# A GRU with a residual on one core: biases spread by products with ones, and x turned by VectorE in 32 x 32 squares

## The chip, the core and the metric

The kernel runs on one core of a Trainium2 chip. The core has TensorE (matrix products, results in PSUM), VectorE, ScalarE and GpSimd (elementwise work; GpSimd does not touch PSUM here), and SyncE (SP), which issues most DMAs. Each engine works through its own list of instructions in order, and waits for others through semaphores. The metric is device microseconds for one execution: the median of three runs before the change is 1333.65 us (1333.27 to 1333.81).

## What is computed

x has 64 rows (batch), 128 steps and 512 features. A GRU runs over the steps; after every fourth step the state goes through one more layer; the states are added to x.

```python
def step(h, inp):
    x_t, prop = inp
    comb = jnp.concatenate([x_t, h], axis=-1)
    z = jax.nn.sigmoid(comb @ Wz + bz)
    r = jax.nn.sigmoid(comb @ Wr + br)
    comb2 = jnp.concatenate([x_t, r * h], axis=-1)
    h_cand = jnp.tanh(comb2 @ Wh + bh)
    h_new = (1.0 - z) * h + z * h_cand
    h_next = jnp.where(prop, jnp.tanh(h_new @ Wp + bp), h_new)
    return (h_next, h_new)
...
x = x + _L0_cond_ref(x, cond_1024, ...)
```

All numbers are float32. The weights are 1024 x 512 for each of r, z and h, and 512 x 512 for the layer after every fourth step.

## The kernel before

**Layout.** The 64 batch rows fill half of the 128 partitions; the 512 features are cut in two halves (S = 2), so a state is a tile of 128 x 256: partition s*64+b, 256 columns of half s. A product takes as stationary operand a 128 x 64 piece of a turned (feature-major) state or x, and streams 256 columns of weights; two such products, one for each half of the columns, run side by side (`products`, L194 in the profile).

**Work of a step.** The recurrent part of a step is a chain: product of h with Wr's lower half (`rc`), sigmoid on ScalarE, r*h on VectorE (`rh`, L742), turning rh on TensorE in 64 x 64 pieces (`turn`, L219) with a copy out of PSUM (`rhT`, L210), product with Wh (`rc` again), tanh (L802), two VectorE operations that make the new state (L803, L808), and turning that (`hT`). Products with Wz (`zp`), the `keep` product (L769) and seeds (`seed`, L411: ScalarE copies the x part of the next step into PSUM, on which the recurrent products accumulate) stand between.

**Work in the gaps.** The x part, x @ W[:512] + b for all three gates, doesn't depend on h. It stands in a `queue` of small units, and `fill(n)` puts n of them wherever the chain would leave TensorE without work. Steps 0 to 3 and the last four are plain products (`plain`, `plain_last`). The others are formed for groups of four steps by two nested levels of a seven-product scheme (`batch`): sums of turned x tiles (`four`, `sum_*`, on GpSimd) times sums of weights (`tw`, `tt`), collected from four PSUM banks (`scratch_q`, `_r`, `_a`, `_x`) by ScalarE and VectorE (`end_1`, `end_2`, L541 to L552), put together by GpSimd (L582, L586, with the biases). `read_out()` places these collecting operations. Which units go where is written out by hand (`PLACES`, `TAIL`).

**How x gets turned.** Steps 0 to 7 are turned on TensorE (`turn_x`) from `xr`, the tile of x to which the state is added later. Steps 8 to 127 take another way, a group of four steps at a time: a load of x with batch rows on partitions (`load_xs`, and `early` for groups 2 and 3), a copy that parts each float32 into its two 16-bit words (`words_x`: GpSimd, L210; ScalarE for groups 2 and 3), a DMA transpose of 16-bit words (`planes_x`, L273), and a ScalarE copy that joins the words again (`join_x`, L283). In a regular period of eight steps two groups pass: joins stand in the steps u = 1, 3, 5, 6, one behind the seeds that follow rh (`join(0)`), one behind `keep` (`join(1)`).

**Start.** SP's ring brings, in this order: half of x of steps 0 and 1, the upper weight halves (`wx`, one piece of Wr and the other half of x through ScalarE's queue), the lower halves (`wh`) of r, of z, x of steps 2 and 3, `wh` of h, x of steps 4 to 7, `early`, Wp. A DMA waits for the one eight places ahead of it to finish. GpSimd's queue brings the state h0 and the biases br, bz, bh, each as two DMAs that repeat one line of 256 numbers on 64 partitions (`load_bias`, L121), after `held`, a copy of one number that waits for x (L130). TensorE first does products of zeros (`idle`), turns steps 0 and 1, then does the x part of steps 0 and 1 gate by gate (R, Z, candidate), turns h0 ahead of the candidate, and enters the loop over steps.

Of the kernel before, what the change touches and what calls it, by code (L numbers as in the profile page):

```python
# [9 lines left out]
F32 = mybir.dt.float32  # L10
BF16 = mybir.dt.bfloat16
U16 = mybir.dt.uint16
# [5 lines left out]
def kernel(  # L18
# [29 lines left out]
    nc = tc.nc  # L48
    B, T, D = x.shape
    H = h0.shape[1]  # L50
    P = 128
    S = 2
    N = H // S
    C = N // P
    K = D // P
    Q4 = 4
# [3 lines left out]
    R, Z, H_ = range(3)  # L60
# [4 lines left out]
    one = ctx.enter_context(tc.tile_pool(name="one", bufs=1))  # L65
    xtp = ctx.enter_context(tc.tile_pool(name="xt", bufs=2))
    mbp = ctx.enter_context(tc.tile_pool(name="mb", bufs=3))
# [8 lines left out]
    ones = const.tile([1, B], F32, name="ones")  # L76
# [5 lines left out]
    wx = const.tile([P, K, 3, H], F32, name="wx")  # L82
# [3 lines left out]
    tw = {n: const.tile([P, S, S, 3, P], F32, name=f"tw_{n}") for n in (2, 3, 4)}  # L86
    tt = const.tile([P, 7, 3, S, 3, P // 2], F32, name="tt")
    gates_in = (Wr, Wz, Wh)
    def load_x(tile_, t0, n, j=0):
        for s in range(S):  # L90
            nc.sync.dma_start(
                out=tile_[s * B : (s + 1) * B, j : j + n, :], in_=x[:, t0 : t0 + n, ts(s, N)]
            )

    def load_w(wt, w, k0, k1, eng):
        eng.dma_start(  # L96
            out=wt[:, k0:k1, :],
            in_=w[k0 * P : k1 * P, :].rearrange("(k p) n -> p k n", p=P),
        )

    xr = {}
# [5 lines left out]
    bias_in = const.tile([P, 4, N], F32, name="bias")  # L107
    new_xr(0)
    for s in range(S):
        (nc.sync, nc.scalar)[s].dma_start(  # L110
            out=xr[0][s * B : (s + 1) * B, 0:2, :], in_=x[:, 0:2, ts(s, N)]
# [7 lines left out]
    def load_bias(i, eng):  # L119
        for s in range(S):  # L120
            eng.dma_start(  # L121
                out=bias_in[s * B : (s + 1) * B, i, :],
                in_=(br, bz, bh, bp)[i][ts(s, N)]
                .rearrange("(o n) -> o n", o=1)
                .broadcast_to([B, N]),
            )


    held = const.tile([1, 1], F32, name="held")
    nc.gpsimd.tensor_copy(held, xr[0][0:1, 0, 0:1])  # L130
    for s in range(S):
        nc.gpsimd.dma_start(out=h_init[s * B : (s + 1) * B, :], in_=h0[:, ts(s, N)])
    for i in (R, Z, H_):
        load_bias(i, nc.gpsimd)
    for i in range(3):
        for k in (0, 2):
            load_w(wh[i], gates_in[i][D:, :], k, k + 2, nc.sync)
        if i == Z:
            load_x(xr[0], 2, 2, 2)

    dummy = const.tile([1, 1], F32, name="dummy")
    nc.scalar.activation(dummy, ones[:, 0:1], AF.Sigmoid)
    new_xr(1)
    load_x(xr[1], 4, 4)
    early = {}
    for g in (2, 3):
        early[g] = mbp.tile([P, 2, 2, 3, P], F32, tag="mb", name=f"early_{g}").rearrange(
            "p a b c d -> p (a b c d)"
        )[:, : Q4 * N].rearrange("p (t n) -> p t n", t=Q4)
    load_x(early[2], 8, 4)  # L150
    load_w(wp, Wp, 0, 4, nc.sync)
    load_bias(3, nc.sync)
    load_x(early[3], 12, 4)


    rc = ps_c.tile([P, 2, N], F32, name="rc")
# [3 lines left out]
    scratch = [ps_c.tile([P, 2 * N], F32, name=f"scratch_{n}") for n in "qrax"]  # L160
# [9 lines left out]
    bias = bias_in.rearrange("p i (c n) -> p c i n", c=C)  # L170

    def cut(ps):
        return ps.rearrange("p (c n) -> p c n", c=C)

    bias0 = bias[:, 0, 0:3, :]
    bias_d = const.tile([P, 3, P], F32, name="bias_d")
# [32 lines left out]
    def copy(eng, dst, src):  # L209
        (eng.copy if eng is nc.scalar else eng.tensor_copy)(dst, src)  # L210

    def turn(src, dst, c, name, eng):


        pt = turn_ps[c][:, :P].bitcast(BF16).rearrange("p (w n) -> p w n", w=2)
        for s in range(S):
            words = src[:, c * P + s * B : c * P + (s + 1) * B].bitcast(BF16)
            for w in range(2):
                nc.tensor.transpose(  # L219
                    pt[s * B : (s + 1) * B, w, :],  # L220
                    words.rearrange("p (n w) -> p w n", w=2)[:, w, :],
                    ident16,
                )
        copy(
            eng,
            dst[:, c, :].bitcast(U16).rearrange("p (n w) -> p n w", w=2),
            pt.bitcast(U16).rearrange("p w n -> p n w"),
        )
# [3 lines left out]


    xT = {}
    xs = {}
    xw = {}
    xv = {}

    def new_xT(g):
        if g not in xT:  # L240
            xT[g] = xtp.tile([P, Q4, C, P], F32, tag="xT", name=f"xT_{g}")

    def turn_x(t, eng=nc.scalar):
        g, i = divmod(t, Q4)
        new_xT(g)
        src = xr[g] if g < 2 else early[g]
        for c in range(C):
            turn(src[:, i, :], xT[g][:, i], c, f"xT_{t}", eng)

    def load_xs(g):  # L250
        if g * Q4 < T:
            xs[g] = one.tile([P, Q4, N], F32, tag="xs", name=f"xs_{g}")
            load_x(xs[g], g * Q4, Q4)

    def words_x(g, i):

        if g * Q4 >= T:
            return
        if g not in xw:
            xw[g] = one.tile([P, Q4, 2, N], U16, tag="xw", name=f"xw_{g}")  # L260
        src = (early if g < 4 else xs)[g]
        copy(
            nc.scalar if g < 4 else nc.gpsimd,
            xw[g][:, i],
            src[:, i, :].bitcast(U16).rearrange("p (n w) -> p w n", w=2),
        )

    def planes_x(g):

        if g * Q4 >= T:  # L270
            return
        xv[g] = one.tile([P, Q4, 2, C, P], U16, tag="xv", name=f"xv_{g}")
        nc.sync.dma_start_transpose(  # L273
            out=xv[g].rearrange("p t w c n -> p (t w c) n"),
            in_=xw[g].rearrange("p t w n -> p (t w n)"),
        )

    def join_x(g, i):

        if g * Q4 >= T:  # L280
            return
        new_xT(g)
        nc.scalar.copy(  # L283
            xT[g][:, i].bitcast(U16).rearrange("p c (n w) -> p w c n", w=2), xv[g][:, i]
        )


# [129 lines left out]
    def fill(n):  # L417
        for _ in range(min(n, len(queue))):
            unit, end = queue.pop(0)
            unit()  # L420
            if end is not None:
                pending.append(end)

    def read_out():
        while pending:
            pending.pop(0)()
# [223 lines left out]
    idle(4)  # L650
    turn_x(1, nc.vector)
    idle(8)
    nc.gpsimd.tensor_sub(bias_d, bias[:, 1, 0:3, :], bias0)
    h = h_init
    hT = new_T("hT", "hT_init")
    both = [plain(0), plain(1)]
    for e in range(3):
        for us in both:
            queue.extend(us[4 * e : 4 * e + 4])
        fill(4)  # L660
        if e == H_:
            read_out()
            seed(R, 0)
            seed(Z, 0)
            seed(H_, 0)
        fill(4)
        if e == Z:
            for c in range(C):
                turn(h, hT, c, "hT_init", nc.vector)
# [4 lines left out]
    for t in range(T):  # L674
        g, j = divmod(t, Q4)
        prop = j == CHUNK - 1 and t < T - 1
        last = t == T - 1
        pair, u = divmod(t - 3, 8)
        even, odd = FIRST + 2 * pair, FIRST + 2 * pair + 1
# [43 lines left out]
        for k in ORDER:  # L723
            product(slots[R], hT, wh[R], k)
        if t < 2:
            if t:
                turn_x(6)
        if t == 1:
            for i in (5, 7):
                sum_inner(i, nc.gpsimd)  # L730
# [20 lines left out]

        for k in ORDER[: 2 if thin else 3]:
            product(slots[Z], hT, wh[Z], k)
        if t == 0:
            turn_x(2)
        rhT = new_T("rhT", f"rhT_{t}")
        for c in range(C):
            turn(rh, rhT, c, f"rhT_{t}", nc.vector)
# [17 lines left out]
        if t == 0:  # L776
            sum_outer()
            for i in (6,):
                sum_inner(i, nc.gpsimd)
                sum_inner_1(i, nc.gpsimd)  # L780
        if t == 1:
            for n in range(4):
                words_x(2, n)
            planes_x(2)
        elif t == 2:
            for n in range(1, 4):
                join_x(2, n)
            for n in range(2):
                words_x(3, n)
        if not thin:  # L790
            fill(places[0])
        if t == 0:
# [7 lines left out]
        for c in range(C):  # L800
# [3 lines left out]
            if last:  # L804
                o = xr[g][:, j, ts(c, P)]
# [2 lines left out]
            nc.vector.tensor_add(h_new[:, ts(c, P)], pc, keep[:, ts(c, P)])  # L808
        if t < T - 2:
            seed(H_, t + 1)  # L810
        if t == 2:
            for n in range(2, 4):
                words_x(3, n)
            planes_x(3)
        read_out()
        fill(places[0] if thin else 5 if places[1] > 6 else 4)
        if t == 1:
# [2 lines left out]
        h = h_new  # L820
# [15 lines left out]
        if prop:  # L836
# [3 lines left out]
            h = two.tile([P, N], F32, tag="hprop", name=f"hprop_{t}")  # L840
# [51 lines left out]
            sum_s12(even + 2)  # L892
        if t == 2:
            pair_right(0, 1, 10)
        if pair >= 0:
            if u in (1, 2):
                for n in range(2):
                    words_x(even + 2, 2 * (u - 1) + n)
            if u in (5, 6):
                for n in range(2):  # L900
                    words_x(odd + 2, 2 * (u - 5) + n)

        if not last:
            nc.gpsimd.tensor_add(xr[g][:, j, :], xr[g][:, j, :], h_new)  # L904
# [4 lines left out]
        n = 0  # L909
        if t >= T - CHUNK:  # L910
            n = {T - 2: 3, T - 1: 1}.get(t, 0)
        elif j == Q4 - 1:
            n = 4
        if n:
            for s in range(S):
                eng = nc.scalar if last and s else nc.sync
                eng.dma_start(
                    out=out[:, t - n + 1 : t + 1, ts(s, N)],
                    in_=xr[g][s * B : (s + 1) * B, j - n + 1 : j + 1, :],
                )  # L920
        if j == 1 and g >= 1 and (g + 1) * Q4 < T:
            new_xr(g + 1)
            load_x(xr[g + 1], (g + 1) * Q4, Q4)
        if t == 0:
            load_xs(4)
        if pair >= 0:
            if u == 3:
                planes_x(even + 2)
                load_xs(odd + 2)
            elif u == 6:  # L930
                planes_x(odd + 2)
                load_xs(even + 4)


# [37 lines left out]
```

## Time and profile before

| | us |
|---|---|
| median of three runs | 1333.65 |
| the profiled execution | 1334.15 |
| its span, first to last instruction | 1332.3 |

| group (line, engine) | count | mean ns | busy us |
|---|---|---|---|
| recurrent product with rhT, L194 TensorE | 2048 | 379 | 246.0 |
| copy of rhT out of PSUM, L210 VectorE | 256 | 420 | 97.6 |
| joining words, L283 ScalarE | 120 | 765 | 91.4 |
| parting words, L210 GpSimd | 112 | 613 | 65.3 |
| adding the state to x, L904 GpSimd | 127 | 728 | 92.5 |
| DMA transposes, issued by SP | 30 | 4.3 us to landing | |

TensorE rows are modelled durations of pipelined matmuls that overlap, so differences between starts are read, not sums of durations. The granted TensorE clock is 0.999 of full speed over the whole span. In the timeline a row has the start in us, the time from the start of the first to the end of the last of the merged instructions, engine, line, operation, output<-inputs, shapes, count, and in brackets the idle time before it and what ended it.

### The profile page before, as it was taken

Reading aid. Unit: us, or ns where it says so; the run is one execution under the profiler, and the core shown is the slowest. Engines: PE = TensorE matmul, PEld = TensorE weight load, DVE = VectorE, ACT = ScalarE, POOL = GpSimd, SP = SyncE. Lnnn points to the kernel's source line nnn. Section 1 sums busy time; section 2 is a strip of 40 time slices with the busy share of each in tenths; the row PEclk is TensorE's granted clock in tenths of the full one; section 3 lists DMA queues with packets and bytes.
Section 4 is the critical chain, followed back from the end, with each engine's and each line's share of the span. In section 5 each row is a group of like instructions: output and inputs, shape, how many; then the busy total and the mean of one; then the engine's idle time right before and its main releaser. Section 6 shows DMA issues by size and latency. Waiting matters only on the chain.

```text
span 1332.3 us, 37617 instructions
## 1 busy us (share of the span) xinstructions
PE 1321.7 (99%) x15320; PEld 1110.8 (83%) x15320; DVE 702.6 (53%) x1870; ACT 635.4 (48%) x1860; POOL 934.9 (70%) x1139
## 2 busy tenths in 40 slices
PE   8999999999999999999999999999999999999998
PEld 5788888888888888888788888888888888888765
DVE  3555555555555555555555555555555555555444
ACT  1554454454544544545444454545545444554433
POOL 4877876777777668776787767786777687767400
PEclk9999999999999999999999999999999999999999
DMA  9322232131221222213122221223212222131300
GB/s 283 55 49 49 49 65 64 33 65 41 57 65 33 66 52 46 65 44 82 37 43 55 64 65 33 59 40 65 65 33 65 49 50 65 33 76 37 98 23 17
DMA packets 119277, 77.79 MB, mean 58 GB/s; under 512 B 65984, under 2 KB 114240, under 8 KB 119104
## 3 DMA queue, kind: packets, MB, share of 16 engines
q1 hardware_dynamic: 118352, 74.14, 24.7%
q8 instruction: 121, 1.98, 0.6%
q10 hardware_dynamic: 496, 0.72, 0.2%
q0 software_dynamic: 256, 0.52, 0.1%
q14 instruction: 52, 0.43, 0.1%
HBM read 42.86 MB, written 16.78 MB: 45 GB/s over the span
## 4 chain that ended last, share of the span: by engine, by line
PE 96%; DMA 2%; DVE 1%; ACT 1%; issue 0%; SPq 0%; DVEq 0%; ACTq 0%
PE rc L194 33%; PE zp L194 20%; PE scratch_q L194 11%; PE scratch_r L194 10%; PE scratch_x L194 10%; PE scratch_a L194 6%; PE turn L219 5%; DMA xr<-in_x_dram 1%; DMA wx<-in_L_cond_Wz_dram 1%; ACT xw L210 0%; ACT xT L283 0%; DVE h L808 0%; DVE turn L803 0%; SPq L96 0%; DVE mb L550 0%
## 5 line engine op out<-in xcount | busy, mean ns | idle before, releaser
L194 PE MATMUL rc<-wh,rhT 128*64 128x256 f32 x2048 | 246.0, 379 | 0.0
L582 POOL TENSOR_TENSOR cp<-mb,mb 128x768 f32<-128x768 f32 x74 | 134.4, 1817 | 102.4 <-ACT rc L411 54.7
L194 PE MATMUL zp<-wh,hT 128*64 128x256 f32 x1536 | 204.3, 379 | 0.0
L194 PEld LDWEIGHTS rc<-wh,rhT 128*64 128x64 f32 x2048 | 168.3, 137 | 40.5
L194 PE MATMUL rc<-wh,hT 128*64 128x256 f32 x1536 | 186.3, 383 | 0.2
L904 POOL TENSOR_TENSOR xr<-xr,h 128x256 f32<-128x256 f32 x127 | 92.5, 728 | 105.3 <-DVE h L808 105.3
L194 PEld LDWEIGHTS rc<-wh,hT 128*64 128x64 f32 x1536 | 121.1, 137 | 36.5 <-issue 9.7
L582 POOL TENSOR_TENSOR cp<-mb 128x768 f32<-128x768 f32 x46 | 83.5, 1815 | 95.1 <-ACT rc L411 93.7
L210 DVE COPY rhT<-turn 128x256 uint16<-128x256 uint16 x256 | 97.6, 420 | 82.2 <-PE turn L219 81.1
L194 PEld LDWEIGHTS zp<-wh,hT 128*64 128x64 f32 x1536 | 118.8, 137 | 25.2
L803 DVE TENSOR_TENSOR turn<-turn,z 128x128 f32<-128x128 f32 x256 | 75.5, 295 | 120.7 <-ACT turn L802 119.0
L741 ACT ACTIVATE turn<-rc 128x128 f32<-128x128 f32 x256 | 55.2, 260 | 171.2 <-issue 111.5
L210 ACT COPY hT<-turn 128x256 uint16<-128x256 uint16 x127 | 47.3, 372 | 165.7 <-DVE hT L210 127.8
L582 POOL TENSOR_TENSOR mb<-mb,mb 128x768 f32<-128x768 f32 x58 | 105.3, 1816 | 9.6 <-DVE mb L552 9.6
L411 ACT COPY rc<-cp 128x256 f32<-128x256 f32 x256 | 96.4, 377 | 26.7 <-DVE cp L436 13.6
L550 DVE TENSOR_TENSOR mb<-scratch_r,cq 128x384 f32<-128x384 f32 (+1 forms) x105 | 58.3, 555 | 92.7 <-ACT cq L549 92.7
L802 ACT ACTIVATE turn<-rc 128x128 f32<-128x128 f32 x256 | 55.5, 260 | 105.3 <-PE rc L194 104.0
L543 DVE TENSOR_TENSOR cx<-scratch_r,cx 128x384 f32<-128x384 f32 (+1 forms) x105 | 58.3, 556 | 88.8 <-ACT cx L541 88.8
L767 ACT ACTIVATE z<-zp 128x256 f32<-128x256 f32 x128 | 49.1, 383 | 94.3 <-PE zp L194 94.2
L283 ACT COPY xT<-xv 128x512 uint16<-128x512 uint16 x120 | 91.4, 765 | 0.0
L808 DVE TENSOR_TENSOR h<-turn,keep 128x128 f32<-128x128 f32 x254 | 74.1, 292 | 15.6 <-DVE turn L803 0.5
L219 PEld LDWEIGHTS <-h 128*64 128x64 bf16 x1016 | 67.6, 110 | 14.0 <-DVE h L808 7.4
(161 smaller groups left out, 3018.0 us busy)
## 6 DMA issues: line engine op xcount, KB each, us to landing
xr<-in_x_dram SPq DMA_DIRECT2D x62, 256.0 KB, 4.1
out_dram<-xr SPq DMA_DIRECT2D x62, 256.0 KB, 3.4
xs<-in_x_dram SPq DMA_DIRECT2D x56, 256.0 KB, 4.2
wx<-in_L_cond_Wz_dram SPq DMA_DIRECT2D x2, 512.0 KB, 8.1
wx<-in_L_cond_Wh_dram SPq DMA_DIRECT2D x2, 512.0 KB, 11.4
wh<-in_L_cond_Wr_dram SPq DMA_DIRECT2D x2, 512.0 KB, 13.2
wh<-in_L_cond_Wz_dram SPq DMA_DIRECT2D x2, 512.0 KB, 15.2
wh<-in_L_cond_Wh_dram SPq DMA_DIRECT2D x2, 512.0 KB, 12.3
```

Of the source, the lines that this page charges most:

```text
L194: nc.tensor.matmul(ps[s * B : (s + 1) * B], lhsT=lhs, rhs=rhs(s), start=start, stop=True, skip_group_check=True,)
L210: (eng.copy if eng is nc.scalar else eng.tensor_copy)(dst, src)
L219: nc.tensor.transpose(pt[s * B : (s + 1) * B, w, :], words.rearrange("p (n w) -> p w n", w=2)[:, w, :], ident16,)
L283: nc.scalar.copy(xT[g][:, i].bitcast(U16).rearrange("p c (n w) -> p w c n", w=2), xv[g][:, i])
L411: nc.scalar.copy(cut(slots[i]), G[t][:, :, i, :])
L543: nc.vector.tensor_add(T2[n][:, :nm], r_ps[:, :nm], T2[n][:, :nm])
L550: nc.vector.tensor_add(blocks()[:, :nm, 0, 1], r_ps[:, :nm], q2[:, :nm])
L582: nc.gpsimd.tensor_add(dst, a, b)
L802: nc.scalar.activation(pc, slots[H_][:, ts(c, P)], AF.Tanh)
L803: nc.vector.tensor_mul(pc, pc, z[:, ts(c, P)])
L808: nc.vector.tensor_add(h_new[:, ts(c, P)], pc, keep[:, ts(c, P)])
L904: nc.gpsimd.tensor_add(xr[g][:, j, :], xr[g][:, j, :], h_new)
```

## The change

Three things change. The biases br, bh and bz come as single lines of 512 numbers (2 KB each) on GpSimd's queue into a corner of `tt` that isn't in use yet; behind the first eight units of the x part, `spread` makes four products of a column of ones with these lines, and ScalarE copies the results to `bias_in`. `held` now waits for a piece of Wr. x of steps 2 and 3 is loaded ahead of Wz's lower half, and step 2 is turned before the Z product instead of behind it. For x of steps 8 to 127, `load_xs` loads pieces of 32 numbers, so that each square of 32 batch rows by 32 features lies in the quarter of the partitions where its turned form belongs, and `join_x` is that one VectorE operation; `words_x`, `planes_x` and the `early` tiles go. There are two such load tiles instead of one, and the load of group 4 moves from step 0 to step 2.

```diff
+    bias_row = tt.rearrange("p a b c d e -> p (a b c d e)")[0:1, : 3 * H].rearrange(
+        "p (i n) -> p i n", i=3
+    )
...
+    for i, b in enumerate((br, bh, bz)):
+        nc.gpsimd.dma_start(out=bias_row[:, i, :], in_=b.rearrange("(o n) -> o n", o=1))
...
-    nc.gpsimd.tensor_copy(held, xr[0][0:1, 0, 0:1])
+    nc.gpsimd.tensor_copy(held, wx[0:1, 1, R, 0:1])
...
-    for i in (R, Z, H_):
-        load_bias(i, nc.gpsimd)
...
-        if i == Z:
+        if i == 0:
             load_x(xr[0], 2, 2, 2)
...
+    def load_xs(g):
+        if g * Q4 < T:
+            xs[g] = one.tile([P, Q4, S * C, 2, 32], F32, tag=f"xs{g % 2}", name=f"xs_{g}")
+            for r in range(4):
+                for bh in range(2):
+                    nc.sync.dma_start(
+                        out=xs[g][ts(r, 32), :, :, bh, :].rearrange("p t k e -> p (t k) e"),
+                        in_=x[ts(bh, 32), g * Q4 : (g + 1) * Q4, :].rearrange(
+                            "b t (k r e) -> r b (t k) e", k=S * C, r=4
+                        )[r],
+                    )
+    load_xs(2)
     load_w(wp, Wp, 0, 4, nc.sync)
     load_bias(3, nc.sync)
-    load_x(early[3], 12, 4)
+    load_xs(3)
...
+    def spread(bank, rows, which):
+        bank = bank.rearrange("p (i n) -> p i n", i=2)
+        n = len(which)
+        for s in range(S):
+            nc.tensor.matmul(
+                bank[s * B : (s + 1) * B, 0:n, :],
+                lhsT=ones,
+                rhs=bias_row[:, rows, ts(s, N)],
+                start=True,
+                stop=True,
+            )
+        for j, i in enumerate(which):
+            nc.scalar.copy(bias_in[:, i, :], bank[:, j, :])
...
     def join_x(g, i):
         if g * Q4 >= T:
             return
         new_xT(g)
-        nc.scalar.copy(
-            xT[g][:, i].bitcast(U16).rearrange("p c (n w) -> p w c n", w=2), xv[g][:, i]
+        nc.vector.transpose(
+            out=xT[g][:, i].rearrange("p c (s b) -> p s c b", s=S),
+            in_=xs[g][:, i].rearrange("p (s c) h e -> p s c (h e)", s=S),
         )
...
-    nc.gpsimd.tensor_sub(bias_d, bias[:, 1, 0:3, :], bias0)
...
         fill(4)
+        if e == R:
+            spread(scratch[3], slice(0, 2), (R, H_))
+            spread(scratch[1], slice(2, 3), (Z,))
+            nc.gpsimd.tensor_sub(bias_d, bias[:, 1, 0:3, :], bias0)
...
         if t < 2:
-            if t:
-                turn_x(6)
+            turn_x((2, 6)[t])
...
-        if t == 0:
-            turn_x(2)
...
-        if t == 1:
-            for n in range(4):
-                words_x(2, n)
-            planes_x(2)
-        elif t == 2:
+        if t == 2:
             for n in range(1, 4):
                 join_x(2, n)
-            for n in range(2):
-                words_x(3, n)
...
-        if t == 0:
+        if t == 2:
             load_xs(4)
         if pair >= 0:
             if u == 3:
-                planes_x(even + 2)
                 load_xs(odd + 2)
             elif u == 6:
-                planes_x(odd + 2)
                 load_xs(even + 4)
```

More of the change, by code (lines that the diff above doesn't have):

```diff
@@ L144 @@
     load_x(xr[1], 4, 4)
[L145 to L150, printed above, removed]
+    xs = {}
+    def load_xs(g):
[10 more added lines that the diff above has]
+    load_xs(2)
     load_w(wp, Wp, 0, 4, nc.sync)
     load_bias(3, nc.sync)
-    load_x(early[3], 12, 4)
+    load_xs(3)
     rc = ps_c.tile([P, 2, N], F32, name="rc")
@@ L234 @@
     xT = {}
-    xs = {}
-    xw = {}
-    xv = {}
     def new_xT(g):
@@ L245, in turn_x @@
         new_xT(g)
-        src = xr[g] if g < 2 else early[g]
+        src = xr[g]
         for c in range(C):
             turn(src[:, i, :], xT[g][:, i], c, f"xT_{t}", eng)
[L250 to L276, printed above, removed]
     def join_x(g, i):
@@ L810 @@
             seed(H_, t + 1)
[L811 to L814, printed above, removed]
         read_out()
@@ L894 @@
             pair_right(0, 1, 10)
[L895 to L901, printed above, removed]
         if not last:
```

## The prediction

> **What bounds the kernel now.** I read the engine row and the chain first, then the windows of the start, TensorE's timeline there, and last VectorE's timeline in a middle step.
>
> ```profile
> PE 1321.7 (99%) x15320; PEld 1110.8 (83%) x15320; DVE 702.6 (53%) x1870; ACT 635.4 (48%) x1860; POOL 934.9 (70%) x1139
> ...
> PE 96%; DMA 2%; DVE 1%; ACT 1%; issue 0%; SPq 0%; DVEq 0%; ACTq 0%
> ```
>
> The chain that ended last is TensorE, 96%. Sixteen matmuls of one 256-column product take 1.73 us, back to back, with no DMA, VectorE or ScalarE row ahead of them. So work removed from GpSimd, ScalarE or the DMA rings is worth nothing in itself; only holes in TensorE's row are. They lie at the start:
>
> ```profile
> 11.32 0.60 PE L194 MATMUL scratch_q<-wx,xT 128*64 128x256 f32 x4
> 12.44 1.52 PE L194 MATMUL scratch_q<-wx,xT 128*64 128x256 f32 x12 [0.52 <-DMA wx<-in_L_cond_Wz_dram]
> ...
> 20.16 1.51 PE L194 MATMUL rc<-wh,hT_init 128*64 128x256 f32 x12 [0.28 <-DMA wh<-in_L_cond_Wr_dram]
> 21.95 0.65 PE L194 MATMUL zp<-wh,hT_init 128*64 128x256 f32 x4 [0.28 <-DMA wh<-in_L_cond_Wz_dram]
> 23.73 1.08 PE L194 MATMUL zp<-wh,hT_init 128*64 128x256 f32 x8 [1.13 <-DMA wh<-in_L_cond_Wz_dram]
> 24.98 0.42 PE L219 MATMUL turn<-ident,xr 128*64 128x128 bf16 x8 [0.17 <-DMA xr<-in_x_dram]
> 25.75 0.58 PE L219 MATMUL turn<-ident,rh 128*64 128x128 bf16 x8 [0.35 <-ACT xT L210]
> ```
>
> Until 26.6 us TensorE waits for weights; the last one, the second half of Wz's recurrent rows, comes at 23.7. From there it is fed. How fast the weights come is in the windows (last two columns: share of the DMA engines, GB/s):
>
> ```profile
> 10.00:12.00 2.00, 1.93 (x18) 1.01 (x14) 0.00 (x0) 0.00 (x0) 0.00 (x0) 1.00 1.06 278
> 12.00:14.00 2.00, 1.56 (x14) 1.06 (x16) 0.00 (x0) 0.00 (x0) 0.00 (x0) 1.00 1.04 261
> 14.00:16.00 2.00, 2.00 (x28) 1.35 (x24) 0.15 (x1) 0.00 (x0) 0.99 (x1) 1.00 1.05 379
> ```
>
> The engines are full throughout, but carry 261 to 278 GB/s while GpSimd's queue (h0 and six bias pieces, issued from 4.3 us, bias_d waiting for them until 14.8) is at work, and 379 after it.
>
> **The biases.** Removed: six 64 KB pieces, 393 KB. At 379 GB/s their bytes alone are 1.0 us of the weights' way. From 8 to 14 us the three windows carried (327+278+261) x 2 = 1732 KB where 379 would have carried 2274: a further 1.4 us lost, three quarters of it the biases' share of that queue (384 of 512 KB), 1.1 us. Together 1.0 to 2.1; I take 1.9. Added ahead of the same transfer: x of steps 2 and 3 now goes before Wz's recurrent rows, 262 KB at the 287 GB/s of 20 to 22 us, 0.9 us. So the 23.7 us become 23.7 - 1.9 + 0.9 = 22.7; with nothing freed 24.6.
>
> The spreading costs TensorE two 512-column and two 256-column products on one row. No such row is in the trace. By columns, at 1.73 us for eight calls of 256, it is 6 x 0.216 = 1.30 us; if one row were cheaper, less, but matmul rows here follow their columns (379 ns at 256, 326 at 192), so 1.3. It stands where the wait at 12.44 is. TensorE's own schedule: 11.33 + 1.30 + 3.46 (Z) + 0.22 (h0 turned) + 3.46 (candidate) + 1.73 (R) + 0.22 (x of step 2, moved ahead) + 0.43 = 22.15 when it asks for the second half. That comes at 22.7; then 0.87 (two of k) + 0.33 (rh turned) + 0.43 = 24.4, against 26.57 before. **Gain 2.2 us**, between 0.3 (nothing freed: 26.3) and 2.8 (TensorE bound: 23.8). ScalarE's three copies of 0.38 us lie between 12 and 14 us, where it was idle (13.6 us before L411); bias_d moves behind them on GpSimd, and the first sum_inner with it, whose results are first used at 45.6 us. Moving step 2's turn puts its two copies (0.65 us) before ScalarE's sigmoid of R; rh is then ready near 23.3, before the turn asks for it. The 0.17 and 0.35 us waits go.
>
> h0 now waits for the first half of Wr, at 7.8 us instead of 4.2. It took 5.8 us from issue to landing; 7.8 + 0.2 + 1.2 (two issues) + 5.2 to 5.8 is 14.4 to 15.0. TensorE asks at 16.1: about 1 us of cover, and every microsecond beyond it stops the whole queue behind.
>
> **x of steps 8 to 127.** Removed: 112 GpSimd copies (65.3 us), 120 ScalarE joins (91.4), 30 DMA transposes, 8 ScalarE copies (4.4). In steps 1 and 2 some of that is on the path:
>
> ```profile
> 45.27 2.18 ACT L210 COPY xw<-early 128x512 uint16<-128x512 uint16 x4
> 47.35 0.47 ACT L541 COPY cx<-scratch_x 128x384 f32<-128x384 f32 x1
> ```
>
> ```profile
> 47.85 0.56 DVE L543 TENSOR_TENSOR cx<-scratch_r,cx 128x384 f32<-128x384 f32 x1 [2.93 <-ACT cx L541]
> ...
> 49.65 0.29 DVE L808 TENSOR_TENSOR h<-turn,keep 128x128 f32<-128x128 f32 x1
> ```
>
> The four copies hold ScalarE's cx, that holds VectorE's for 2.93 us (second fence) and one addition more, and these hold h; TensorE's turns begin at 49.46 and 49.99 where its products had ended at 49.23, in all 0.85 us lost. With cx two microseconds earlier h follows tanh, at 49.1: **0.75 us**. In step 2 two copies and three joins (62.1 to 65.0) hold cq, three VectorE additions and h: hole of 0.41 + 0.10 before the turns at 67.66 and 68.19: **0.45 us**. The 0.22 us wait in step 3 (L550) stands behind rhT in VectorE's order and stays.
>
> Added: 120 transposes of 128x256 f32 on VectorE. Nearest rows: SBUF additions of 128x384 take 547 ns and of 128x768 957, so 1.07 ns a column and 137 fixed: 0.41 us; if the operation took two passes, 0.68. In all 49 us on an engine at 53%. What counts is where they stand: one behind rh, one behind keep.
>
> ```profile
> 169.54 0.49 DVE L742 TENSOR_TENSOR rh<-turn,hprop 128x128 f32<-128x128 f32 x2 [0.83 <-ACT turn L741]
> 170.66 0.76 DVE L210 COPY rhT<-turn 128x256 uint16<-128x256 uint16 x2 [0.62 <-PE turn L219]
> 171.90 0.42 DVE L769 TENSOR_TENSOR keep<-zp,hprop 128x256 f32<-128x256 f32 x1 [0.48 <-ACT zp L768]
> 173.61 0.30 DVE L803 TENSOR_TENSOR turn<-turn,z 128x128 f32<-128x128 f32 x1 [1.29 <-ACT turn L802]
> ```
>
> Behind keep 1.29 us are free. Behind rh it is 0.62, and queued behind the transpose is rhT, which the candidate's product needs: that product starts at 171.30, 0.21 us after rhT's first half. So a transpose up to **0.8 us** is hidden, one of 0.41 leaves 0.4. This place comes 57 times (two steps for each of 28 groups, and step 4).
>
> A rule speaks against it. Two-input SBUF work on VectorE beside GpSimd costs: GpSimd's addition at L334 takes 1.00 us alone and 1.76 beside VectorE's two L326, which average 1.35 where L320 of the same size takes 0.95, 0.8 us on the two. The Trainium skill (SBUF — State Buffer, Who interferes with whom) says why: the two share a port pair, and a VectorE instruction that uses it blocks until GpSimd's ends; but with one SBUF input outside the two-port modes it doesn't. The transpose has one input. By the rule's exempt side it costs 0.41 and the sum gets 0; by the row it costs 0.41 + 0.8 = 1.2, and 57 x 0.4 = 23 us come on top. VectorE's rh (one SBUF input) keeps 281 to 292 ns beside a GpSimd that is 70% busy, so I take 0.
>
> Its loads: eight per group instead of two, 4096 packets of 128 B. The main ring's 118352 packets took 24.7% of 16 engines, 0.247 x 16 x 1332.3 / 118352 = 44 ns each, so 256 per engine are 11.4 us a group. The skill (DMA: Bandwidth & Descriptors, Specifications) gives 512 B as the least size at full rate, with read-modify-write below; doubled, 23 us. Two groups come in 81 us, six or more steps ahead, so the sum is 0 by both. At the start the first group follows x of steps 4 to 7 (landed by 30 to 32) and lands at 43, by the rule at 55; VectorE's first transpose is due near 51, in front of rhT, which has 5.7 us of idle time ahead. Wp behind it lands by 47, or 59, and is due at 77. On SP the group of steps 16 to 19 moves from step 0 to step 2, in front of the first output store, which waits for GpSimd anyway.
>
> **Sum.** 2.2 + 0.75 + 0.45 = 3.4 us of the span of 1332.3. The profiled execution took 1334.15 (1.85 around the span), so 1330.75 of that; the runs' median lies 0.5 lower, so **1330.3**.
>
> **Rivals.** (1) The start gives little: the freed ring time isn't passed to Wz, or h0 lands a microsecond late. Gain 0.3 to 1.2 at the start, 1.5 to 2.4 in all: 1331.3 to 1332.2. For it: the ring is also slow (287 GB/s) at 20 us without biases. Against: the drop to 261 and the return to 379 fall on GpSimd's queue. 25%. (2) The transpose passes 0.8 us at the 57 places: at 1.2 us 23 - 3.4 gives 1353; at 0.9 it is 5.7 - 3.4, 1336. For it: the L334 rows, and no transpose in the trace. Against: rh's steady duration. 13%, a late first load in it. (3) Gains hold, but small VectorE delays (a transpose of 0.5 to 0.8) reach the short holes before h in steady steps: result within 2 us of before, 4%, counted with (1).
>
> **Numbers.** Forecast 58% (1329.0 to 1331.0). A difference of 0.2% is 2.7 us, the least this measurement tells from none; the forecast is just above it, so of its 58% and of (1)'s 29% I give faster 59%, same 27%, slower 14%. Range: 1328.8 (start TensorE bound, all holes closed) to 1334.3.
>
> **What would show it.** Right: the spread at 11.3 us for about 1.3, no wait on Wz's input rows, Wz's recurrent half near 22.7, step 0's fill near 24.4, turns of step 1 without a hole, transposes near 0.41 us, TensorE's steps after step 4 as long as before. Wrong: transposes over 0.8 us with TensorE waiting for rhT, or TensorE waiting for h_init.

## The result, and the profile after

The changed kernel takes 1330.9 us (median of 20 runs, 1330.35 to 1331.35); the kernel before, run on the same chip between them, 1333.72 us (20 runs, 1332.73 to 1336.55). The ratio is 0.9977, with a 95% interval of 0.9971 to 0.9983: 2.8 us, 0.23%, faster. The profiled executions have spans of 1329.2 and 1332.3 us, 3.1 us apart; the one before lay 0.4 us above its median and the one after at it, hence 2.8 against 3.1. The forecast was 1330.3.

First the page's engine row, the chain of waits, the load and the main ring, as answers to the lines shown of before:

```profile
PE 1320.8 (99%) x15328; PEld 1108.5 (83%) x15328; DVE 746.4 (56%) x1990; ACT 555.0 (42%) x1735; POOL 871.3 (66%) x1024
...
q1 hardware_dynamic: 166352, 58.42, 20.4%
...
PE 99%; DMA 0%; DVE 0%; issue 0%; ACT 0%; SPq 0%; DVEq 0%; ACTq 0%
...
xs<-in_x_dram SPq DMA_DIRECT2D x240, 64.0 KB, 2.8
```

ScalarE lost 80 us of work and GpSimd 64, VectorE gained 44, and the time moved by 3. TensorE was the chain before at 96% and is now at 99%: what went were the 2% of DMA and the 1% each of VectorE and ScalarE in it. All waits of TensorE that are left (total, times, longest):

```profile
PE rc L212 <- DVE zeros L73: 1.2, 1, 1.2
PE scratch_q L224 <- DMA wx<-in_L_cond_Wr_dram: 1.0, 1, 1.0
PE turn L249 <- DVE h L803: 0.4, 2, 0.2
PE scratch_r L224 <- DVE mb L550: 0.2, 1, 0.2
```

No wait for Wz stands in the list any more. The timeline of TensorE in the start shows no idle bracket from the spread on:

```profile
11.58 1.07 PE L195 MATMUL scratch_x<-tt,ones 1*64 1x512 f32 x4
12.49 0.60 PE L195 MATMUL scratch_r<-tt,ones 1*64 1x256 f32 x4
13.02 1.95 PE L224 MATMUL scratch_q<-wx,xT 128*64 128x256 f32 x16
...
20.20 1.90 PE L224 MATMUL rc<-wh,hT_init 128*64 128x256 f32 x16
...
22.15 1.47 PE L224 MATMUL zp<-wh,hT_init 128*64 128x256 f32 x12
23.45 0.50 PE L249 MATMUL turn<-ident,rh 128*64 128x128 bf16 x8
23.79 0.60 PE L224 MATMUL zp<-wh,hT_init 128*64 128x256 f32 x4
24.22 3.62 PE L224 MATMUL scratch_q<-wx,xT 128*64 128x256 f32 x32
```

The fill of step 0 starts at 24.22 (26.57 before). All of Wz's lower half has landed at 21.31; TensorE begins its product at 22.15 and comes to the later of the two pieces, the one that landed at 21.31, at 22.58, so that piece is 1.27 us early. To see where the 3.1 us come from, I take the start of the candidate's product with rhT in each step, in both traces, and subtract (rounded last):

| product with rhT of step | before | after | earlier by |
|---|---|---|---|
| 0 | 31.97 | 29.63 | 2.34 |
| 1 | 46.20 | 43.83 | 2.36 |
| 2 | 63.95 | 61.34 | 2.61 |
| 3 | 77.62 | 74.53 | 3.08 |
| 4 | 90.08 | 87.00 | 3.09 |
| 48 | 536.50 | 533.45 | 3.05 |
| 127 | 1325.33 | 1322.09 | 3.24 |

So the start gave 2.34, the end of step 1 gave 0.25, that of step 2 0.47, and the 57 places with a transpose behind rh cost nothing that shows: from step 4 to step 127 the distance stays between 3.05 and 3.24. In step 1 a hole is left; the timeline of all engines there:

```profile
44.05 0.48 ACT L541 COPY cx<-scratch_x 128x384 f32<-128x384 f32 x1 [1.08 <-PE scratch_x L224]
...
45.84 0.43 ACT L797 ACTIVATE turn<-rc 128x128 f32<-128x128 f32 x2 [0.93 <-PE rc L224]
46.13 0.30 DVE L798 TENSOR_TENSOR turn<-turn,z 128x128 f32<-128x128 f32 x1 [0.55 <-ACT turn L797]
...
46.86 0.28 PE L249 MATMUL turn<-ident,xr 128*64 128x128 bf16 x4
47.00 0.29 DVE L803 TENSOR_TENSOR h<-turn,keep 128x128 f32<-128x128 f32 x1
...
47.34 0.31 PE L249 MATMUL turn<-ident,xr 128*64 128x128 bf16 x4 [0.20 <-DVE h L803]
47.61 0.30 PE L249 MATMUL turn<-ident,h 128*64 128x128 bf16 x4
```

ScalarE's cx waits for its own product only, so the copies that held it are gone. What is late now is the recurrent chain itself: from the end of the candidate's product (45.73) through tanh, the multiplication and the addition to the second half of h (47.29) it takes 1.56 us, and TensorE has 1.30 us of products to put beside it (45.56 to 46.86). The turn that waits there, at 47.34, is one of x and doesn't read h: it is written to the PSUM tile in which tanh and the additions of the same half work (`turn_ps` and `act_ps` in the kernel).

Last, the new operation (least, median and largest ns over 120), and one of the 57 places, on VectorE's timeline:

```profile
L282 DVE STREAM_TRANSPOSE xT<-xs x120: 398/434/447, 51.3 to 1242.9; 128x256 f32<-128x256 f32 x120
```

```profile
166.48 0.49 DVE L745 TENSOR_TENSOR rh<-turn,hprop 128x128 f32<-128x128 f32 x2 [0.83 <-ACT turn L744]
167.03 0.45 DVE L282 STREAM_TRANSPOSE xT<-xs 128x256 f32<-128x256 f32 x1
167.60 0.76 DVE L240 COPY rhT<-turn 128x256 uint16<-128x256 uint16 x2
```

The transpose takes 0.43 us and nothing longer than 0.45 occurs, beside a GpSimd that is at work 66% of the time.

### The profile page after: what moved, and what is told of

It is laid out like the page before. It is cut to its first block, busy times and chain, and to the rows that moved or that the text cites. A ratio compares the mean times of both kernels' runs of the same rounds, so it can differ in the third digit from the quotient of the medians.

```text
span 1329.2 us, 37725 instructions
## 1 busy us (share of the span) xinstructions
PE 1320.8 (99%) x15328; PEld 1108.5 (83%) x15328; DVE 746.4 (56%) x1990; ACT 555.0 (42%) x1735; POOL 871.3 (66%) x1024
## 4 chain that ended last, share of the span: by engine, by line
PE 99%; DMA 0%; DVE 0%; issue 0%; ACT 0%; SPq 0%; DVEq 0%; ACTq 0%
PE rc L224 34%; PE zp L224 21%; PE scratch_q L224 11%; PE scratch_r L224 11%; PE scratch_x L224 11%; PE scratch_a L224 6%; PE turn L249 5%; DMA wx<-in_L_cond_Wr_dram 0%; DVE turn L798 0%; DVE h L803 0%; PE scratch_x L195 0%; ACT turn L797 0%; SPq L114 0%; DVE xr L801 0%; DVE rhT L240 0%
## 5 line engine op out<-in xcount | busy, mean ns | idle before, releaser
L768 ACT ACTIVATE z<-zp 128x256 f32<-128x256 f32 x128 | 49.1, 383 | 134.0 <-PE zp L224 134.0
L249 PE MATMUL turn<-ident,h 128*64 128x128 bf16 x1016 | 77.6, 220 | 0.3 <-DVE h L803 0.2
## 6 DMA issues: line engine op xcount, KB each, us to landing
wh<-in_L_cond_Wr_dram SPq DMA_DIRECT2D x2, 512.0 KB, 11.4
```

The costliest lines, as they stand in the source:

```text
L249: nc.tensor.transpose(pt[s * B : (s + 1) * B, w, :], words.rearrange("p (n w) -> p w n", w=2)[:, w, :], ident16,)
```

## The experiments

My theory: 2.3 of the 3.1 us are ring bytes (the biases') that no longer stand ahead of Wz, the rest two holes; transposes are free because they fit behind rh. The rivals: the start's gain is the new order (x of step 2 ahead) or the later start of h0; and the steady steps only look free because something else hides a longer transpose. Below, "step 0" is the start of its product with rhT, 29.63 us in the kernel after.

**e1_bias_back: the biases (and h0's early start) as before, the rest as after.**

```diff
-    for i, b in enumerate((br, bh, bz)):
-        nc.gpsimd.dma_start(out=bias_row[:, i, :], in_=b.rearrange("(o n) -> o n", o=1))
...
-    nc.gpsimd.tensor_copy(held, wx[0:1, 1, R, 0:1])
+    nc.gpsimd.tensor_copy(held, xr[0][0:1, 0, 0:1])
...
+    for i in (R, Z, H_):
+        load_bias(i, nc.gpsimd)
...
-            spread(scratch[3], slice(0, 2), (R, H_))
-            spread(scratch[1], slice(2, 3), (Z,))
```

> The bias part undone: six broadcast pieces on GpSimd's queue ahead of which nothing waits but x, no spread on TensorE; all else as in the changed kernel. Theory (the ring's bytes): Wz's recurrent half comes near 24.5 us instead of 21.3, so TensorE waits about 3 us for it although it has 1.5 us less to do; step 0's product with rhT starts near 31.5 (29.6 with the change, 32.0 before); span 1331 us. Rival (the start's gain came from moving x of steps 2 and 3 and its turn): TensorE, rid of the spread, is 1.5 us earlier, step 0's product near 28.1, span 1327.7.

Measured: 1333.15 us (1332.47 to 1333.58), ratio 0.9995 (0.9985 to 1.0004), step 0 at 31.34. The number fits, but its profile shows another cause. TensorE's timeline:

```profile
10.02 2.08 PE L224 MATMUL scratch_q<-wx,xT 128*64 128x256 f32 x12 [2.74 <-DMA wx<-in_L_cond_Wr_dram]
11.89 3.06 PE L224 MATMUL scratch_a<-wx,xT 128*64 128x256 f32 x16
14.78 1.90 PE L224 MATMUL scratch_q<-wx,xT 128*64 128x256 f32 x16
```

and its windows (columns: TensorE's busy time, granted clock, share of the DMA engines, GB/s):

```profile
10.00:11.00 1.00, 0.98 (x8) 0.92 1.04 277
11.00:12.00 1.00, 1.00 (x8) 0.50 1.05 297
...
14.00:15.00 1.00, 1.00 (x11) 0.88 1.05 385
```

The piece of Wr that ScalarE's queue brings landed at 9.98 instead of 7.59, and sixteen matmuls took 2.9 us from start to start instead of 1.73: the granted clock was 0.50 from 11 to 14 us. Wz, at 23.24, was not waited for. This run proves nothing for the theory.

**e2_bias_alone: the kernel before with the bias part alone** (the lines, `spread`, `held`; x turned as before, order as before).

> The kernel before with the bias part alone. Theory: Wz's half near 20.5, no wait for it; the turn of step 2 behind the Z product still costs its 0.4 us; step 0's product with rhT near 30.0 (32.0 before), holes of steps 1 and 2 (0.85 and 0.5 us) as before, span 1330.3. Rival: near 31.7, span 1332.

Measured: 1332.37 us (1332.06 to 1333.27), ratio 0.9991 (0.9982 to 1.0), step 0 at 30.04 against 31.97 before. Wz's second half landed at 21.10, where it had been 23.69, and the product with it has no wait (21.95 and 23.73 in the kernel before had):

```profile
21.77 1.46 PE L214 MATMUL zp<-wh,hT_init 128*64 128x256 f32 x12
```

The holes of steps 1 and 2 stay: the distance to the kernel after grows from 0.42 us (step 0) through 0.68 (step 2) to 1.14 (step 3), and is still 1.14 at step 4. The bias part alone gives 1.93 of the start's 2.34 us.

**e3_order_back: x of steps 2 and 3 behind Wz, step 2 turned behind the Z product**, the rest as after.

```diff
-        if i == 0:
+        if i == Z:
             load_x(xr[0], 2, 2, 2)
...
-            turn_x((2, 6)[t])
+            if t:
+                turn_x(6)
...
+        if t == 0:
+            turn_x(2)
```

> The changed kernel with x of steps 2 and 3 loaded behind Wz's lower half again, and step 2 turned behind three quarters of the Z product again. Theory: Wz comes earlier still but is not waited for; the turn of step 2 and its ScalarE copy stand between Z and rh's turn, 0.3 to 0.6 us; span 1329.6. Rival (the move is what pays at the start): span 1331 or more.

Measured: 1331.76 us (1331.18 to 1332.28), ratio 0.9985 (0.9975 to 0.9994); step 0 at 30.47. Of the 0.84 us, 0.28 are the first product, which began at 8.26, behind the later of Wr's two pieces (8.21; 7.94 in the kernel after). The other 0.56 are the turn between the Z product and the turn of rh:

```profile
23.50 0.39 PE L249 MATMUL turn<-ident,xr 128*64 128x128 bf16 x8
24.25 0.58 PE L249 MATMUL turn<-ident,rh 128*64 128x128 bf16 x8 [0.36 <-ACT xT L240]
```

The turn of rh waits for ScalarE, which is copying x of step 2 out of the same bank. So the order gives about half a microsecond, and by a PSUM bank that comes free, not by Wz. With e2 this accounts for the start: 1.93 and 0.56, less 0.16 for the first product (at 7.98, before at 7.82), are 2.33 of the 2.34 us.

**e9_one_ring and e10_one_ring_bias_back: the biases' bytes, without Wr's chance.** Both bring both pieces of Wr through SP's ring; e10 has the biases back as in e1 in addition.

```diff
-            load_w(
-                wx[:, :, i, :], gates_in[i], k, k + 2, nc.scalar if (i, k) == (R, 2) else nc.sync
-            )
+            load_w(wx[:, :, i, :], gates_in[i], k, k + 2, nc.sync)
```

> The changed kernel with both pieces of Wr's upper half on SP's queue, in a row (in the changed kernel one goes through ScalarE's). Theory (where the two rings share the engines it is chance which piece of Wr comes last, and profiles showed 7.8 to 10.1 us for it; one ring keeps the order): TensorE's first product at 7.3 to 8.0 in each profile, a narrow spread of times, median 1330 to 1331. Rival (one queue issues too slowly or carries less): first product at 8.5 or later, median 1331.5 or more.

> The same, with the biases again as six broadcast pieces on GpSimd's queue and no spread. Theory (the pieces take 1.9 us of the ring's time from the weights): Wr isn't late now, so TensorE, 1.5 us ahead without the spread, asks for Wz's recurrent half near 20.5 and gets it near 23: step 0's product with rhT 0.8 to 1.8 us later than in the kernel with one ring alone. Rival (in the run before this one it was Wr's late piece and the clock that cost, not the biases' bytes): 0.5 to 1.5 us earlier than it.

Measured: e9 1330.8 us (1330.51 to 1331.08), ratio 0.9972 (0.9961 to 0.9983), step 0 at 29.83; e10 1333.23 us (1332.71 to 1334.17), ratio 0.9991 (0.9981 to 1.0), step 0 at 31.47. TensorE's timeline in e10:

```profile
12.36 1.52 PE L222 MATMUL scratch_q<-wx,xT 128*64 128x256 f32 x12 [1.03 <-DMA wx<-in_L_cond_Wz_dram]
...
20.95 1.51 PE L222 MATMUL rc<-wh,hT_init 128*64 128x256 f32 x12 [1.16 <-DMA wh<-in_L_cond_Wr_dram]
...
23.12 0.65 PE L222 MATMUL zp<-wh,hT_init 128*64 128x256 f32 x4 [0.43 <-DMA wh<-in_L_cond_Wz_dram]
24.49 1.08 PE L222 MATMUL zp<-wh,hT_init 128*64 128x256 f32 x8 [0.72 <-DMA wh<-in_L_cond_Wz_dram]
```

Wr's upper half costs a wait of only 0.48 us here and the clock is full, and TensorE waits for Wz's upper half, Wr's lower and Wz's lower, although 1.5 us of spreading are gone from its list. In e9 it waits for none of these three; its product with Wz's lower half runs through:

```profile
22.36 1.47 PE L222 MATMUL zp<-wh,hT_init 128*64 128x256 f32 x12
```

The second half of Wz lands at 24.45 (22.03 in e9): 2.4 us for the six pieces, 393 KB, and for h0, which in e10 is not held back either. This is the shown part of the theory: what GpSimd's queue brings beside the weights, not the spread, decided the start. No run holds h0 back alone, so its later start and the six pieces are not separated; its own 131 KB land ahead of Wz in every run.

**e7_spread_early and e11_one_ring_spread_early: the spread before the first product.** The bias lines go through ScalarE's queue ahead of the weights, and the spread stands where TensorE still waits for Wr; e11 has one ring besides.

```diff
+    for i, b in enumerate((br, bh, bz)):
+        nc.scalar.dma_start(out=bias_row[:, i, :], in_=b.rearrange("(o n) -> o n", o=1))
...
-    idle(8)
+    idle(2)
+    spread(scratch[3], slice(0, 2), (R, H_))
+    spread(scratch[1], slice(2, 3), (Z,))
```

> The changed kernel with the three bias lines on ScalarE's queue ahead of its piece of Wr, and the spread before the first product, in the place of products of zeros. Theory (TensorE waits nowhere behind 8 us, so the spread's 1.5 us are on the path now): the first product stays within 0.4 us of 8.0, the rest moves 1.1 to 1.5 us earlier, span 1327.7 to 1328.1. Rival (Wr's piece behind three more issues comes 1 to 2 us later): span 1329 to 1330.

> One ring for Wr, the bias lines on ScalarE's queue behind its half of x, the spread before the first product. Theory (the early spread failed because Wr's piece stood behind the lines' issues and TensorE's clock fell while it waited): lines land by 6, Wr by 8, no wait of TensorE over 1 us, full clock; 1.2 to 1.5 us less than with one ring alone. Rival (the lines themselves, in 128-byte packets among the weights, are late or delay Wr; or one-row products don't keep the clock): half clock again, 1333.

Measured: e7, a single run, 1333.75 us, step 0 at 32.62, 3.0 us later than after. Wr's piece on ScalarE's queue, now issued behind three lines, landed at 10.13; the clock had fallen to half during the wait for it, at 9.1 us by the shares below. Its windows (first column behind the length: TensorE's busy time; the one before the last two: granted clock):

```profile
8.00:9.00 1.00, 0.44 (x4) 0.00 (x0) 0.00 (x0) 0.40 (x2) 0.52 (x1) 1.00 1.06 399
9.00:10.00 1.00, 0.00 (x0) 0.00 (x0) 0.00 (x0) 0.00 (x0) 0.47 (x1) 0.55 1.04 401
10.00:12.00 2.00, 1.83 (x10) 1.07 (x12) 0.00 (x0) 0.00 (x0) 0.00 (x0) 0.50 1.06 355
...
15.00:16.00 1.00, 1.00 (x8) 0.61 (x6) 0.00 (x0) 0.00 (x0) 0.92 (x2) 0.54 1.09 327
16.00:18.00 2.00, 2.00 (x20) 1.26 (x18) 0.00 (x0) 0.00 (x0) 1.92 (x3) 1.00 1.09 266
```

e11: 1331.26 us (1330.51 to 1331.81), ratio 0.9976 (0.9966 to 0.9986). The spread costs nothing (6.35 and 7.26 us), the first products run from 7.79 without a wait, and step 0 comes at 29.38, only 0.45 us before e9's. TensorE turns x of step 2 1.75 us ahead of e9 (20.38 against 22.13) and gives 1.3 of it back waiting for Wz's lower half, ahead of 21.05 and of 22.40:

```profile
PE zp L222 <- DMA wh<-in_L_cond_Wz_dram: 1.0, 2, 0.7
```

So in the kernel after, where the piece of Wz that is wanted last is 1.27 us early, at most about that much of the spread's 1.5 us can be won. The median shows no gain at all: the 0.45 us are gone by the last step (1322.46 against e9's 1322.26), and why was not followed.

**e4_turn_twice and e5_turn_thrice: how much does the place behind rh hide?** The transposes at the 57 places are made two and three times.

```diff
+        for _ in range(times):
+            nc.vector.transpose(
...
-                join_x(even + 2, 2 * (u - 5) + n)
+                join_x(even + 2, 2 * (u - 5) + n, 1 if n else 2)
```

> Each transpose that stands behind rh (57 of 120) is done twice. Theory (0.8 us of cover there, a transpose takes 0.43): two take 0.87, so 0 to 0.1 us comes through at each of 57 places: 0 to 4 us more than the changed kernel, span 1329 to 1333. Rival (VectorE's work is free wherever it stands): no difference. Rival (any VectorE work there delays TensorE already): 57 x 0.4 = 23 us.

> Each transpose behind rh is done three times. Theory: 1.30 us against 0.8 of cover, 0.4 to 0.5 at each of 57 places: 23 to 28 us more than the changed kernel, span 1352 to 1357. Rival (free wherever it stands): no difference.

Measured: e4 1340.7 us (1340.52 to 1341.54), ratio 1.0054 (1.0039 to 1.0069). From step 4 on it falls behind by 9.5 us, 0.17 at each place, more than the 0 to 0.1 expected. e5, a single run: 1367.62 us, 36.6 us or 0.64 at each, where 0.4 to 0.5 were expected. VectorE's timeline in e4, at the place shown above:

```profile
168.45 0.93 DVE L283 STREAM_TRANSPOSE xT<-xs 128x256 f32<-128x256 f32 x2
169.30 0.72 DVE L240 COPY rhT<-turn 128x256 uint16<-128x256 uint16 x2
```

The second transpose runs straight into rhT, which starts 0.85 us after the pair does; 0.17 of it shows, so the place hides about 0.70 us, not the 0.8 of the prediction. With three, rhT starts 1.33 us after them (168.91 to 170.24 in e5) and 0.64 shows, again 0.69 hidden. In e5's list of TensorE's waits they stand:

```profile
PE rc L224 <- ACT zp L770: 17.1, 40, 0.5
PE rc L224 <- DVE rhT L240: 6.9, 16, 0.8
```

The first line names ScalarE's last sigmoid of zp, but the product doesn't need it: in the kernel after the product starts at 168.25, and that sigmoid only at 168.42. What holds the product in both lines is rhT behind the three transposes. With one transpose of 0.43, as in the kernel after, about 0.27 us are to spare at each of 57 places: the free result is no accident, and something over 0.70 would not have been free.

**e6_two_holes, e12_holes, e14_two_holes_timed: the holes that are left.** In step 3 the readers of four banks stand behind rhT; both e6 and e12 place `read_out()` ahead of the turn of rh. For step 1, e6 turns x of step 7 behind h; e12 puts one more unit of the x part before the turn, and by the same number in `places` one unit instead of two between the two turns of h. The first three pieces below are e6's, the last is e12's, which has the first too.

```diff
+        if t == 3:
+            read_out()
         rhT = new_T("rhT", f"rhT_{t}")
...
-        if t == 1:
-            turn_x(7)
-            sum_raw34(1)
         h = h_new
...
+        if t == 1:
+            turn_x(7)
+            sum_raw34(1)
...
-            places = (8, 6)
+            places = (8, 7)
```

> The changed kernel with step 7's x turned behind h of step 1 instead of ahead of it, and in step 3 the collecting operations read out ahead of rhT's copies. Theory (the hole left in step 1 is the turn of x waiting for VectorE's h in the same PSUM tile; the hole in step 3 is L550 standing behind rhT): 0.3 to 0.4 us each, span 1328.4. Rival (the chain from tanh to h has no cover there at all, whatever stands first): step 1's hole stays, span 1328.8 to 1329.2.

> The changed kernel with step 3's read-out moved ahead of rhT's copies, as in the run on two holes, and in step 1 one more unit of the x part between the candidate's product and h's turn. Theory (step 1's chain from the product to h takes 1.56 us and has 1.30 of products beside it; a fifth unit is 0.33): 0.2 to 0.3 us in step 1 and 0.4 in step 3, median 1330.3. Rival (the unit moved is missed behind h's turn): step 1 gives 0.

> The kernel after with two moves and nothing left out: step 7's squares are turned behind step 1's turn of h instead of ahead of it, and step 3's read_out() comes ahead of the turn of rh instead of behind it. One look at it had given 0.07 in step 1 and 0.41 in step 3. Theory: the two add up and stay, since nothing behind step 3 waits: median 1330.3 to 1330.6 against the kernel after's 1330.9, each against the same kernel before. Rival: the gain is smaller than the scatter of the start (Wr's piece lands at another time in each execution), and the median stays at 1330.9 within 0.2.

Measured: in step 3 both give 0.41 us, the hole before `scratch_r` is gone. In step 1 e6 gives 0.07 and e12 loses 0.32. Each trades one wait for another, as TensorE's timelines show, e6 first and e12 second:

```profile
48.28 0.31 PE L249 MATMUL turn<-ident,xr 128*64 128x128 bf16 x4 [0.36 <-ACT hT L240]
```

```profile
48.08 0.31 PE L249 MATMUL turn<-ident,h 128*64 128x128 bf16 x4 [0.29 <-ACT xT L240]
```

Turns of h and of x share two PSUM pieces, and whichever is second waits for ScalarE to empty the first. Times: e6 1330.55 us (a single run), e12 1331.32 us (1331.04 to 1331.72), ratio 0.9978 (0.9968 to 0.9988). e6's kernel timed as e14: 1330.81 us (1330.38 to 1331.23), ratio 0.9975 (0.9966 to 0.9985). In e14's trace step 4 is 0.43 us earlier than after's, of which 0.27 are left in the last third, and the span is 1328.9; the medians don't tell it from the kernel after. No version that measurably beats it was found.

## Why the prediction was right, step by step

**What bounds the kernel.** Right. 144 us of work left ScalarE and GpSimd, and only what had been holes in TensorE's row moved the time.

**The bytes of the biases.** The mechanism was right, and two terms were mis-sized, both so that Wz was put later than it came. The freed way was put at 1.9 us; e2 moved Wz's second half by 2.59 (23.69 to 21.10) and e10 by 2.42. x of steps 2 and 3 ahead of it was put at 0.9; between e2 and the kernel after Wz lands 0.21 later. That second figure is less than the scatter: e5, e6, e12 and e14 start just as the kernel after does, and there Wz landed at 22.06, 21.57, 21.43 and 22.56. The first is more: with the six pieces it never came before 23.24 (e1). So Wz came at 21.31, not 22.7, and TensorE's own list became the bound, the case the prediction gave as its best. The reading behind the 1.9, that the ring is slow while GpSimd's queue is at work, was too simple. Windows of the kernel after are still slow, with six bias pieces gone:

```profile
10.00:12.00 2.00, 2.00 (x18) 1.03 (x16) 0.00 (x0) 0.00 (x0) 0.00 (x0) 1.00 1.06 389
12.00:14.00 2.00, 2.00 (x18) 0.97 (x16) 0.00 (x0) 0.92 (x3) 0.29 (x1) 1.00 1.06 296
14.00:16.00 2.00, 2.00 (x22) 1.35 (x20) 0.00 (x0) 0.00 (x0) 1.92 (x3) 1.00 1.07 336
16.00:18.00 2.00, 2.00 (x28) 1.37 (x26) 1.15 (x3) 0.00 (x0) 1.92 (x3) 1.00 1.09 263
```

h0, now landing at 13.55 and 14.22, lies in the slow window from 12 us. In the one from 16 us GpSimd's queue has nothing under way: x of steps 2 and 3, which lands at 18.39 and 18.77, is on SP's ring there, and of 339 packets 140 are under 2 KB. So the rate falls with x's small pieces too. How much of the 2.4 to 2.6 us is bytes and how much is rate, no run separates.

**The spread.** Put at 1.30 us by columns; 1.53 (the end of the last product's turn at 11.49 to Z at 13.02). The columns were right; the 0.23 us more lie where the shape changes (0.09 ahead of 11.58, 0.05 ahead of 12.49, 0.10 ahead of 13.02, by columns). The start's gain of 2.34 against 2.2 is the sum of these errors: Wz earlier by 1.4 than put, up to the bound of TensorE's list, and that list longer by 0.23 and by the first product's 7.98 instead of 7.82. That it came so close is in part luck: the errors about Wz and about the list had opposite senses.

**h0.** Landing at 14.22 against 14.4 to 15.0, wanted at 16.5: right, no wait.

**Step 1's hole.** The step that was wrong: "With cx two microseconds earlier h follows tanh, at 49.1: 0.75 us". It gave 0.25. h did follow tanh, but I did not ask what the recurrent chain needs when nothing holds it: 1.56 us, against 1.30 of products. Taking ScalarE's copies away left the chain itself as the next late one, 0.26 of the hole by these two figures; the turn of x meets it in the PSUM tile that they share, and e6 and e12, which close this wait, each open another at such a tile. What the hole would be without the sharing no run shows. **Step 2's hole**, 0.45 put, 0.47 measured. **Step 3's** 0.22 stayed as said; e6 shows it was worth 0.41.

**The transposes.** 0.41 put by the row of additions, 0.434 measured; cover of 0.8 put, 0.70 measured (e4). No cost at 57 places, as forecast. The rule of the Trainium skill in SBUF — State Buffer, Who interferes with whom, by its exempt side, fits; the dearer row (two-input additions stretched beside GpSimd) doesn't carry over to this operation, since 120 transposes spread by 398 to 447 ns only.

**The loads of 128-byte pieces.** Put at 44 ns a packet and 11.4 us a group, first landing at 43. The first group landed between 27.4 and 31.6 us: 256 packets for each engine in the 4.6 us from the DMA before it at 27.00, 18 ns each. The 44 was a mean over packets of 626 B (74.14 MB in 118352). It stayed off the path by either figure. The Trainium skill (DMA: Bandwidth & Descriptors, Specifications) gives 512 B as the least size at full rate but no factor below it; the doubling was the prediction's own estimate. A lower rate does show: 104 GB/s from 27 to 31.6 us, with the engines 61% busy, against 389 from 20 to 22.

**The rivals.** The first (start gives little) fell with e10, the second (transposes past their cover) with e4 in both directions: no cost at one, 0.17 at two. The third (small delays of VectorE in the steady steps) is not seen: the distance is 3.09 us at step 4 and 3.24 at step 127. **The sum**: 2.34 + 0.25 + 0.47 = 3.06 of the span, put at 3.4. The median fell by 2.8, and the interval of the ratio (0.9971 to 0.9983) leaves out 1. Of the 0.6 us between 1330.9 and the forecast, about 0.3 are this sum; the rest is mainly that the median was put 0.5 below the profiled execution, which held for the kernel before (0.43) and not for the one after (0.04).

## What to carry to other kernels

Where TensorE is the chain from the first weight on, transfers beside the weights can cost as much as products (here 2.4 us with the six pieces and h0's early start): move constants as one line and spread them on TensorE, and check whether that makes the weights early enough to matter no further. When a stall's cause is removed, cost the gain as the distance to what is late next, measured from that chain's own rows, before booking the whole hole. To learn how much a "free" place hides, put the operation there two and three times.

## What was not expected of the hardware

**The clock.** In e1 a wait of 2.74 us (7.28 to 10.02) and in e7 one of 1.73 us (8.44 to 10.17) came with a fall of the granted clock from 1.00 to 0.50, in e1 0.8 us after work had resumed, in e7 during the wait; sixteen matmuls then took 2.9 to 3.3 us instead of 1.73. In e4 a wait of 2.04 us (7.43 to 9.47) at the same place left it full. By the shares in the windows (a mean of 0.92 is full clock for 0.84 of the microsecond) the half clock lasted from 10.84 to 14.24 us in e1 and from 9.10 to 15.92 in e7: 3.4 and 6.8 us. The Trainium skill (TensorE: Matmul & The Clock Gate, What's actually happening) names an activity window of about 3.4 us that runs freely and isn't reset by the kernel; one and two such windows agree with these durations, and the phase could explain that e4's wait, cut by a border, cost nothing and e1's did. It doesn't explain e7. There the clock fell 0.66 us after the wait began. If a window ended at the fall, no more than that of the wait lies in it, while of e4's wait at least half, 1.02 us, lies in one window wherever the border is. What stands ahead of e7's wait are 1.44 us of products on one row (6.35 to 7.79); e11 has the same rows, followed by full products without a wait, and kept its clock. This points to products on one row counting for little as activity. It wasn't tried by itself.

**Two rings.** Wr's piece on ScalarE's queue landed between 6.30 us (e12) and 9.98 (e1) without a change in how it was issued; with both pieces on SP's ring the second came at 8.57, 7.62 and 8.40 us (e9, e10, e11). It came after 9 us in e1 and e4 alone of these runs, and there its issue on ScalarE took 0.87 us and that of the other piece on SP 0.57, where the other runs have 0.61 and 0.82 to 0.84. The two issues start within 0.05 us of each other, and which piece gets ahead seems to be settled there, by chance. That chance is of the size of the effects looked for here, which is why e9 and e10 were needed.
